# Moving conv inputs to an idle GpSimd and projection ahead of conv, in a kernel of attention and dynamic filters

## Chip, cores, metric

One core of one Trainium2 chip. The metric is the device time of one execution in microseconds (us), the median of several executions. A ratio is the mean time of one kernel's fast runs over the mean of the other's fast runs of the same rounds, so it is not quite the ratio of the medians quoted beside it. The call that a difference of two per cent is "faster" or "slower" uses a 95% interval.

## The reference

Four images of 256 channels, 48 x 48 pixels, fp32. Cut to what matters:

```python
# layer 0: group norm -> 3x3 conv 256->256 -> batch norm, relu -> q,k,v -> attention (8 heads,
# 2304 tokens) -> projection
x = x + _L0_conv_ref(_gn(x), ...)

# layer 1: group norm -> guidance -> five dynamic branches -> 1x1 conv -> batch norm
def _L1_conv_ref(x, W_cat, W_scale, gamma, beta):
    guidance = _conv(x, W_cat, pad=1)                       # 45 channels
    outs = [x]
    for i, d in enumerate((1, 6, 12, 24, 36)):
        w = softmax(guidance[:, 9*i : 9*(i+1)], axis=1)
        outs.append(_dyn_branch(x, w, d))                   # 9 shifted taps, each weighted per pixel
    y = _conv(concatenate(outs, axis=1), W_scale, pad=0)
    return (y - mean) * rsqrt(var + EPS) * gamma + beta     # mean, var over batch and pixels
x = x + _L1_conv_ref(_gn(x), ...)
```

## The kernel before

The 3x3 conv is computed in a transformed form: for each of six indices `i` a transformed weight `u_i` and a transformed input; the image is worked on in two halves `g`. The inputs come in three stages (0: indices 1 and 2; 1: indices 3 and 4; 2: indices 0 and 5). The conv is a generator that yields after each matmul, so other parts of the kernel can use it as filler: `run(n)` issues conv work worth `n`. This fixes the program order on every engine.

```python
        ORDER = (1, 2, 3, 4, 0, 5)
        ...
            def inputs(stage, g):                       # all on DVE
                ...
                if stage == 0:
                    for h in range(NH):
                        axpy(v4[5][:, h], d[2][:, h], -4.0, d[4][:, h])
                        axpy(v4[0][:, h], d[1][:, h], -4.0, d[3][:, h])
                    tt(v[1], v[5], v[0], ALU.add)
                    tt(v[2], v[5], v[0], ALU.subtract)
                elif stage == 1: ...
            ahead = weights(ORDER[0])
            for at, i in enumerate(ORDER):
                u = ahead
                if at + 1 < len(ORDER):
                    ahead = weights(ORDER[at + 1])
                for g in range(2):
                    if at == 0:
                        inputs(0, g)
                    if at in (1, 3):
                        inputs((at + 1) // 2, g)
                    for o in range(NH):
                        ...  # six matmuls, yield after each, then outputs(i, g, o, m)
```

The joint phase of image b (dynamic filters of b, conv and q/k/v of b + 1 as filler) opens so:

```python
            run(3500)                                   # conv work first
            while chunk < NCK:
                project(b, chunk, ao, ..., norm)        # projection of attention, norm statistics
                chunk += 1
            run(3000)
            for _ in norm.finish(misc):                 # small steps of the norm
                run(1500)
            for h in range(NH):
                normalize(inside(gn, h), inside(gn, h), norm.mean, norm.rstd, h)
                run(2000)
            for got in weights(0):                      # guidance, softmax, transposes
                if not got:
                    run(1300)
            # then the taps, with conv and q/k/v as filler
```

## Time and profile before

| | before |
|---|---|
| time, median (range) | 3212.65 us (3209.42 to 3214.46, 4 runs) |
| first conv matmul | 37.0 us |
| end of the first conv with q/k/v | 156.4 us |
| opening of a joint phase: last attention sums to first tap (three of them) | 67.21, 67.09, 67.15 us |
| tap stage after it | 297.0, 296.4, 294.3 us |

How to read the rows: a joint phase begins for us where TensorE forms the last sums of the softmax ("den") of the attention before it. "pg" is the guidance conv, "wb" the first tap, "pc" a conv matmul, "pp" the projection. The opening is den to first wb, and it has two halves, den to pg and pg to wb.

The table of stretches for the two halves of the first opening, kernel before; columns as the prediction gives them (length, busy time and instructions of PE, weight load, DVE, ACT, POOL, clock, DMA share, GB/s):

```profile
555.70:589.90 34.20, 24.16 (x86) 16.76 (x86) 16.20 (x35) 3.08 (x6) 0.00 (x0) 0.80 0.25 81
589.90:622.90 33.00, 33.00 (x165) 21.07 (x165) 13.98 (x27) 5.10 (x10) 0.00 (x0) 1.00 0.09 26
```

In the first half TensorE idles for 10 us; in the second it has no gap at all. GpSimd does nothing in either.

### The profile page before, as it was taken

How to read it: one execution, taken by the hardware profiler on the slowest of the kernel's cores; microseconds unless marked ns; L12 is line 12 of the kernel's file. 1: busy time of each engine (PE TensorE's matmuls, PEld its weight loads, DVE VectorE, ACT ScalarE, POOL GpSimd, SP SyncE). 2: the span in 40 equal slices, each digit the busy share in tenths (PEclk: the TensorE clock that was granted, in tenths of full speed). 3: DMA queues.
4: the chain of work that ended last, by engine and by line, in shares of the span. 5: the costliest groups of instructions: out<-in, count | busy, mean ns of one | idle time of the engine just before them, and what ended most of it. 6: DMA issues, size and time to landing. Idle time of an engine off the chain costs nothing.

```text
span 3208.1 us, 42897 instructions
## 1 busy us (share of the span) xinstructions
PE 2892.8 (90%) x17494; PEld 1301.4 (41%) x17494; DVE 2441.5 (76%) x2422; ACT 1514.4 (47%) x1724; POOL 1005.5 (31%) x752
## 2 busy tenths in 40 slices
PE   5999999979899999898999999987989999978873
PEld 4722223555542223455562222455554222334441
DVE  5488888487768888668767888848776888858785
ACT  0388877111148888301117887711114888840002
POOL 4000000189940000058980000018894000007672
PEclk9999999999999999999999999999999999988876
DMA  3400000100030000100003000010001000040005
GB/s 147 98 1 6 6 11 8 58 25 20 10 69 6 6 1 11 40 25 32 23 6 65 6 6 11 6 55 15 10 6 40 6 6 1 11 158 5 10 10 212
DMA packets 74701, 100.25 MB, mean 31 GB/s; under 512 B 51952, under 2 KB 62720, under 8 KB 71424
## 3 DMA queue, kind: packets, MB, share of 16 engines
q1 hardware_dynamic: 73696, 92.02, 9.8%
q0 software_dynamic: 800, 5.41, 0.4%
q8 instruction: 139, 2.28, 0.3%
q14 instruction: 66, 0.54, 0.1%
HBM read 64.39 MB, written 33.03 MB: 30 GB/s over the span
## 4 chain that ended last, share of the span: by engine, by line
PE 72%; DVE 12%; POOL 6%; ACT 4%; issue 4%; DMA 2%; SPq 0%; DVEq 0%; POOLq 0%; ACTq 0%
PE se L852 21%; PE num L882 18%; PE py L1141 10%; PE pc L766 7%; POOL cat L1225 6%; PE pg L1024 5%; DVE prod L1222 4%; PE wb L1201 3%; PE den L904 3%; ACT p L861 3%; PE pq L794 2%; PE pp L953 2%; DVE acc L897 2%; PE pv L813 1%; DVE yt L723 1%
## 5 line engine op out<-in xcount | busy, mean ns | idle before, releaser
L1225 POOL TENSOR_TENSOR cat<-cat,prod 128x752 f32<-128x752 f32 (+8 forms) x720 | 971.8, 1358 | 2113.7 <-DVE prod L1222 1155.5
L861 ACT ACTIVATE p<-se 128x1024 f32<-128x1024 f32 x1296 | 1259.0, 1026 | 282.2 <-PE se L852 243.8
L897 DVE TENSOR_TENSOR acc<-acc,p 128x2048 f32<-128x2048 f32 x504 | 1154.6, 2291 | 113.5 <-ACT p L861 74.7
L852 PE MATMUL se<-q,k 32*128 32x512 f32 (+1 forms) x5760 | 803.8, 594 | 12.0 <-ACT p L861 8.8
L1222 DVE TENSOR_TENSOR prod<-wb,pad 128x768 f32<-128x768 f32 (+7 forms) x768 | 551.6, 746 | 203.7 <-PE wb L1201 135.7
L882 PE MATMUL num<-p,vT 128*32 128x512 f32 (+1 forms) x5760 | 696.4, 563 | 8.8 <-ACT no L900 7.4
L1201 PE MATMUL wb<-w,pick 90*128 90x384 f32 (+3 forms) x888 | 434.4, 530 | 98.1 <-DVE prod L1222 86.8
L852 PEld LDWEIGHTS se<-q,k 32*128 32x128 f32 x5760 | 291.3, 183 | 529.0 <-issue 425.4
L1141 PE MATMUL py<-cat,wsc 128*128 128x384 f32 x960 | 397.0, 543 | 43.0 <-POOL cat L1225 43.0
L882 PEld LDWEIGHTS num<-p,vT 128*32 128x32 f32 x5760 | 121.7, 108 | 488.4 <-issue 440.2
L1201 PEld LDWEIGHTS wb<-w,pick 90*128 90x128 f32 x888 | 176.7, 203 | 261.9 <-DVE prod L1222 150.2
L1141 PEld LDWEIGHTS py<-cat,wsc 128*128 128x128 f32 x960 | 197.5, 212 | 152.0 <-POOL cat L1225 52.6
L766 PE MATMUL pc<-cv_q,u 128*128 128x288 f32 x576 | 165.1, 426 | 36.8 <-DMA u<-u_d 21.8
L766 PE MATMUL pc<-cv_k,u 128*128 128x288 f32 x576 | 164.0, 422 | 8.8 <-DVE cv_k L695 8.7
L1024 PE MATMUL pg<-pad,wcat 128*45 128x384 f32 x864 | 153.9, 499 | 2.6 <-DVE pad L582 2.4
L1216 DVE TENSOR_TENSOR cat<-wb,pad 128x768 f32<-128x768 f32 x114 | 108.2, 949 | 45.5 <-PE wb L1201 45.5
L766 PEld LDWEIGHTS pc<-cv_q,u 128*128 128x128 f32 x576 | 112.5, 201 | 69.9 <-issue 41.3
L794 PE MATMUL pq<-hid,wqkv 128*128 128x384 f32 x384 | 136.1, 486 | 0.0
L897 DVE TENSOR_TENSOR acc<-p,p 128x2048 f32<-128x2048 f32 x36 | 82.5, 2292 | 66.1 <-ACT p L861 66.1
L1156 ACT COPY y<-py 128x768 f32<-128x768 f32 x24 | 19.2, 798 | 231.5 <-PE py L1141 231.5
L766 PEld LDWEIGHTS pc<-cv_k,u 128*128 128x128 f32 x576 | 110.3, 197 | 37.9 <-issue 10.0
L710 ACT ACTIVATE hid<-yt,bn_t_f,bn_s 128x288 f32<-128x288 f32 x64 | 39.7, 626 | 167.7 <-DVE yt L728 97.7
(161 smaller groups left out, 1524.7 us busy)
## 6 DMA issues: line engine op xcount, KB each, us to landing
pad<-in_x SPq DMA_DIRECT2D x14, 1152.0 KB, 15.0
u<-u_d SPq DMA_DIRECT2D x18, 768.0 KB, 4.4
x_d<-pad SPq DMA_DIRECT2D x48, 192.0 KB, 2.5
y_d<-y SPq DMA_DIRECT2D x24, 384.0 KB, 2.7
xst<-in_x SPq DMA_DIRECT2D x36, 192.0 KB, 2.4
u_d<-u SPq DMA_DIRECT2D x6, 768.0 KB, 3.7
y<-y_d SPq DMA_DIRECT2D x2, 2304.0 KB, 13.8
x<-x_d SPq DMA_DIRECT2D x2, 2304.0 KB, 21.4
```

The source lines that it names most:

```text
L766: nc.tensor.matmul(m, u[:, h, kx, o * P : (o + 1) * P], halves[g][:, h, place[i], :, kx : kx + WW], start=(h == 0 and kx == 0), stop=(h == ...
L794: nc.tensor.matmul(pq[:, :CH], wqkv[:, i, s, g * P : (g + 1) * P], hid[:, i, cols], start=(i == 0), stop=(i == NH - 1),)
L852: nc.tensor.matmul(ss[j // 2][:, j % 2, at : at + n], k_[r, g, m * P : (m + 1) * P], q[r, g, q0 : q0 + n], start=True, stop=True,)
L861: nc.scalar.activation(p[:, 2 * pair : 2 * pair + 2, :], ss[pair], AF.Exp, scale=QS)
L882: nc.tensor.matmul(st["num"][r, at : at + n], vT[:, m, g * P + j * D : g * P + (j + 1) * D], p[:, j, at : at + n], start=(m == 0 and not s ...
L897: nc.vector.tensor_tensor(st["acc"], other, p, ALU.add)
L1024: nc.tensor.matmul(pg[64 * s : 64 * s + NG, :CH], wcat[:, i, k, :], window(gn, i, (c + s) * R, k // 3 - 1, k % 3 - 1), start=(i == 0 and k ...
L1141: nc.tensor.matmul(py[c][:, o, :CH], wsc[:, n * NH + i, o * P : (o + 1) * P], rhs(i), start=(n == 0 and i == 0), stop=(last and i == NH - 1),)
L1201: nc.tensor.matmul(pw[:, : nr * WW], pick[:, k : k + 1].to_broadcast([2 * NG, P]), w[:, l0 * WW : l1 * WW], start=True, stop=True,)
L1216: nc.vector.tensor_tensor(accv, wb, src, ALU.mult)
L1222: nc.vector.tensor_tensor(pv, wb, src, ALU.mult)
L1225: eng.tensor_tensor(dst, dst, pv, ALU.add)
```

## The change

Its intent: let the idle GpSimd make the conv inputs in the openings; put projection and norm, which lead to the guidance, ahead of the conv filler; load conv weights ahead of need; let DVE instead of GpSimd make the transformed weights at the start; take the norm's small steps off DVE. The diff, cut to its core:

```diff
 class Norm: finish()
-                nc.vector.tensor_copy(mean, pm[:, :NH])
-                nc.vector.tensor_tensor(d2, mv[:, :, 0], mean, ALU.subtract)
-                nc.vector.tensor_tensor(d2, d2, d2, ALU.mult)
-                nc.vector.tensor_tensor(d2, d2, mv[:, :, 1], ALU.add)
+                nc.scalar.copy(mean, pm[:, :NH])
+                for h in range(NH):
+                    nc.scalar.activation(d2[:, h : h + 1], mv[:, h, 0:1], AF.Square,
+                                         bias=mean[:, h : h + 1], scale=-1.0)
                 yield
-                nc.tensor.matmul(pv[:, :NH], gmat, d2, start=True, stop=True)
+                nc.tensor.matmul(pv[:, :NH], gmat, mv[:, :, 1], start=True, stop=False)
+                nc.tensor.matmul(pv[:, :NH], gmat, d2, start=False, stop=True)
 transformed weights, made once (made_from)
-                eng = nc.gpsimd          # eng.tensor_tensor(...)
+                nc.vector.tensor_tensor(...)
 conv inputs
+                tt = (nc.vector if b == 0 else nc.gpsimd).tensor_tensor
+                mul = nc.scalar.mul
                 if stage == 0:
-                    (four fused multiply-adds, two adds, on DVE)
+                    mul(v[0], d[2], 4.0)
+                    mul(v[5], d[1], 4.0)
+                    tt(v[0], d[4], v[0], sub)
+                    tt(v[5], d[3], v[5], sub)
+                    tt(v[1], v[0], v[5], add)
+                    tt(v[2], v[0], v[5], sub)
                 elif stage == 1:
+                    tt(v[6], d[3], d[1], sub)
+                    tt(v[5], d[4], d[2], sub)
+                    mul(v[6], v[6], 2.0)
+                    tt(v[3], v[5], v[6], add)
+                    tt(v[4], v[5], v[6], sub)
                 else:
+                    tt(v[0], d[0], d[2], sub)
+                    mul(v[6], v[6], 2.0)
+                    mul(v[0], v[0], 4.0)
+                    tt(v[0], v[0], v[5], add)
+                    tt(v[5], d[5], d[3], sub)
+                    tt(v[5], v[5], v[6], sub)
 when the inputs are issued: {(position in ORDER, half): [(stage, half)]}
+            if b == 0:
+                when = {(at, g): [(j, g)] for j, at in enumerate((0, 1, 3)) for g in range(2)}
+            else:
+                when = {(0, 0): [(0, 0)], (0, 1): [(0, 1), (1, 0), (1, 1)],
+                        (1, 0): [(2, 0), (2, 1)]}
 opening of a joint phase
-            run(3500)
             while chunk < NCK:
                 project(...)
             run(3000)
-            for _ in norm.finish(misc):
-                run(1500)
+            for at, _ in enumerate(norm.finish(misc)):
+                run((600, 1500)[at])
             for h in range(NH):
                 normalize(inside(gn, h), inside(gn, h), norm.mean, norm.rstd, h)
-                run(2000)
+            run(3500)
             for got in weights(0):
                 if not got:
-                    run(1300)
+                    run(800)
```

Left out: the first weights of the next conv are loaded before the joint phase begins, and the last phase keeps one tile in a buffer that has become free.

More of the change, by code (lines that the diff above doesn't have):

```diff
@@ L528, in conv_preact_kernel @@
         name="act", bufs=1
-    ) as act, tc.manual_schedule():
+    ) as act, tc.tile_pool(name="u", bufs=2) as upool, tc.manual_schedule():
         def image_of(src, b):
@@ L607, in finish, with shift_of @@
                 nc.tensor.matmul(pm[:, :NH], gmat, mv[:, :, 0], start=True, stop=True)
-                nc.vector.tensor_copy(mean, pm[:, :NH])
-                nc.vector.tensor_tensor(d2, mv[:, :, 0], mean, ALU.subtract)
-                nc.vector.tensor_tensor(d2, d2, d2, ALU.mult)
-                nc.vector.tensor_tensor(d2, d2, mv[:, :, 1], ALU.add)
+                nc.scalar.copy(mean, pm[:, :NH])
+                for h in range(NH):
+                    nc.scalar.activation(
+                        d2[:, h : h + 1], mv[:, h, 0:1], AF.Square, bias=mean[:, h : h + 1],
+                        scale=-1.0,
+                    )
                 yield
                 pv = psum_tile(f"pv_{self.name}")
-                nc.tensor.matmul(pv[:, :NH], gmat, d2, start=True, stop=True)
+                nc.tensor.matmul(pv[:, :NH], gmat, mv[:, :, 1], start=True, stop=False)
+                nc.tensor.matmul(pv[:, :NH], gmat, d2, start=False, stop=True)
                 rstd_of(rstd, pv[:, :NH])
                 self.mean, self.rstd = mean, rstd
+            def shift_of(self):
                 self.shift = small.tile([P, NH], F32, tag="gshift", name=f"gshift_{self.name}")
                 nc.vector.scalar_tensor_tensor(
-                    out=self.shift, in0=mean, scalar=-1.0, in1=rstd, op0=ALU.mult, op1=ALU.mult
+                    out=self.shift, in0=self.mean, scalar=-1.0, in1=self.rstd, op0=ALU.mult,
+                    op1=ALU.mult,
                 )
@@ L634, in conv_preact_kernel, with taken @@
         TN = TJ * WW
-        def taken_from(pool):
-            def load(i):
-                u = pool.tile([P, NH, 3, C], F32, tag="u", name=f"u_{i}")
-                nc.sync.dma_start(out=u, in_=u_d[i])
-                return u
-            return load
+        def taken(i):
+            u = upool.tile([P, NH, 3, C], F32, tag="u", name=f"u_{i}")
+            nc.sync.dma_start(out=u, in_=u_d[i])
+            return u
         def made_from(wc, pool):
             w = [wc[:, :, 3 * j : 3 * j + 3, :] for j in range(3)]
-            t = pool.tile([P, NH, 3, C], F32, tag="ut", name="u_t")
+            t = pool.tile([P, NH, 3, C], F32, tag="ut", name="u_t", bufs=1)
             def make(i):
-                u = pool.tile([P, NH, 3, C], F32, tag="u", name=f"u_{i}")
-                eng = nc.gpsimd
+                u = upool.tile([P, NH, 3, C], F32, tag="u", name=f"u_{i}")
                 if i == 1:
-                    eng.tensor_tensor(t, w[0], w[2], ALU.add)
+                    nc.vector.tensor_tensor(t, w[0], w[2], ALU.add)
                 if i == 3:
-                    eng.tensor_scalar(t, w[0], 0.25, None, ALU.mult)
-                    eng.tensor_tensor(t, t, w[2], ALU.add)
+                    nc.vector.tensor_tensor(t, w[0], w[2], ALU.add)
+                if i in (1, 3):
+                    nc.vector.tensor_tensor(u, t, w[1], ALU.add)
+                if i in (2, 4):
+                    nc.vector.tensor_tensor(u, t, w[1], ALU.subtract)
+                if i == 2:
+                    nc.scalar.mul(w[0], w[0], 0.25)
                     nc.scalar.mul(w[1], w[1], 0.5)
-                if i in (1, 3):
-                    eng.tensor_tensor(u, t, w[1], ALU.add)
-                if i in (2, 4):
-                    eng.tensor_tensor(u, t, w[1], ALU.subtract)
                 if i == 0:
-                    nc.scalar.mul(u, w[0], -1.5)
+                    nc.scalar.mul(u, w[0], -6.0)
                 if i == 5:
@@ L669, in made_from, with conv @@
             return make
-        def conv(b, gn, psum_tile, weights, pool, hid):
+        def conv(b, gn, psum_tile, weights, ready, pool, hid):
             halves = [
-                act.tile([P, NH, 6, TJ, PADW], F32, tag=tag, name=f"cv_{b}_{tag}")
+                act.tile([P, NH, 7, TJ, PADW], F32, tag=tag, name=f"cv_{b}_{tag}")
                 for tag in ("q", "k")
@@ L678, in conv @@
             S12, D12, S34, D34 = range(4)
-            place = {1: 1, 2: 2, 3: 3, 4: 4, 0: 1, 5: 2}
             def inputs(stage, g):
-                v = [halves[g][:, :, i].rearrange("p h t w -> p h (t w)") for i in range(6)]
-                v4 = [halves[g][:, :, i] for i in range(6)]
+                v = [halves[g][:, :, i] for i in range(7)]
                 d = [
@@ L687, in inputs @@
                 ]
-                tt, stt = nc.vector.tensor_tensor, nc.vector.scalar_tensor_tensor
-                def axpy(out, x, a, y):
-                    stt(out=out, in0=x, scalar=a, in1=y, op0=ALU.mult, op1=ALU.add)
+                tt = (nc.vector if b == 0 else nc.gpsimd).tensor_tensor
+                mul = nc.scalar.mul
+                add, sub = ALU.add, ALU.subtract
                 if stage == 0:
-                    for h in range(NH):
-                        axpy(v4[5][:, h], d[2][:, h], -4.0, d[4][:, h])
-                        axpy(v4[0][:, h], d[1][:, h], -4.0, d[3][:, h])
-                    tt(v[1], v[5], v[0], ALU.add)
-                    tt(v[2], v[5], v[0], ALU.subtract)
-                elif stage == 1:
-                    tt(v4[5], d[4], d[2], ALU.subtract)
-                    tt(v4[0], d[3], d[1], ALU.subtract)
-                    axpy(v[3], v[0], 2.0, v[5])
-                    axpy(v[4], v[0], -2.0, v[5])
-                else:
-                    tt(v4[1], d[0], d[2], ALU.subtract)
-                    axpy(v[1], v[1], 4.0, v[5])
-                    tt(v4[2], d[5], d[3], ALU.subtract)
-                    axpy(v[2], v[0], -4.0, v[2])
+                    mul(v[0], d[2], 4.0)
[4 more added lines that the diff above has]
+                    tt(v[2], v[0], v[5], sub)
+                elif stage == 1:
+                    tt(v[6], d[3], d[1], sub)
[3 more added lines that the diff above has]
+                    tt(v[4], v[5], v[6], sub)
+                else:
+                    tt(v[0], d[0], d[2], sub)
[4 more added lines that the diff above has]
+                    tt(v[5], v[5], v[6], sub)
             def relu(g, o, r, y):
@@ L749, in outputs @@
                     result(3, m, None, d12)
-            ahead = weights(ORDER[0])
+            if b == 0:
+                when = {(at, g): [(j, g)] for j, at in enumerate((0, 1, 3)) for g in range(2)}
+            else:
+                when = {
+                    (0, 0): [(0, 0)], (0, 1): [(0, 1), (1, 0), (1, 1)], (1, 0): [(2, 0), (2, 1)]
+                }
+            ahead = ready
             for at, i in enumerate(ORDER):
                 u = ahead
-                if at + 1 < len(ORDER):
-                    ahead = weights(ORDER[at + 1])
                 for g in range(2):
-                    if at == 0:
-                        inputs(0, g)
-                    if at in (1, 3):
-                        inputs((at + 1) // 2, g)
+                    for stage, gg in when.get((at, g), ()):
+                        inputs(stage, gg)
+                    if g == 0 and at + 1 < len(ORDER):
+                        ahead = weights(ORDER[at + 1])
                     for o in range(NH):
@@ L768, in conv @@
                                     u[:, h, kx, o * P : (o + 1) * P],
-                                    halves[g][:, h, place[i], :, kx : kx + WW],
+                                    halves[g][:, h, i, :, kx : kx + WW],
                                     start=(h == 0 and kx == 0),
@@ L776, in conv, with conv_qkv @@
                         yield MM * TN / CH
-        def conv_qkv(b, gn, psum_tile, weights, pool):
+        def conv_qkv(b, gn, psum_tile, weights, ready, pool):
             hid = keep("h", f"hid_{b}")
-            yield from conv(b, gn, psum_tile, weights, pool, hid)
+            yield from conv(b, gn, psum_tile, weights, ready, pool, hid)
             q, k_ = keep("q", f"q_{b}"), keep("k", f"k_{b}")
@@ L1288, in merged @@
                 pass
+        u_next = None
         for b in range(B + 1):
@@ L1302, in conv_preact_kernel @@
                 if b < B:
-                    if b == 0:
-                        for _ in norm0.finish(psc):
-                            pass
-                        for h in range(NH):
-                            normalize(inside(pads[0], h), rows_of(x_first[:, h, :]), norm0.mean,
-                                      norm0.rstd, h)
-                    weights = taken_from(work1)
+                    weights = taken
                     if b == 0:
@@ L1319, in conv_preact_kernel @@
                         weights = made_from(wc, work1)
+                        rest = norm0.finish(psc)
+                        next(rest)
+                        u_next = weights(ORDER[0])
+                        for _ in rest:
+                            pass
+                        for h in range(NH):
+                            normalize(inside(pads[0], h), rows_of(x_first[:, h, :]), norm0.mean,
+                                      norm0.rstd, h)
                     nn, stats = None, iter(())
@@ L1324, in conv_preact_kernel @@
                     other = merged(
-                        conv_qkv(b, pads[b % 2], psc, weights, work1), 40000.0, 4000.0,
+                        conv_qkv(b, pads[b % 2], psc, weights, u_next, work1), 40000.0, 4000.0,
                         stats,
@@ L1361, in conv_preact_kernel @@
                 load_pad(b + 1)
+                u_next = taken(ORDER[0])
                 fin = [None]
@@ L1368, in step @@
                         )
-                    next(fin[0], None)
+                    if next(fin[0], fin) is fin:
+                        nn.shift_of()
                 def piece(h, r0, b=b, nn=nn):
@@ L1392, in conv_preact_kernel @@
         with tc.tile_pool(name="last", bufs=1) as last:
-            t = [last.tile([P, NH, N], F32, tag=f"last{j}", name=f"last{j}") for j in range(3)]
-            nc.sync.dma_start(out=t[2], in_=y_d[B - 2])
-            again[B - 2] = t[2], again[B - 2][1]
+            t = [last.tile([P, NH, N], F32, tag=f"last{j}", name=f"last{j}") for j in range(2)]
+            nc.sync.dma_start(out=t[1], in_=y_d[B - 2])
+            again[B - 2] = t[1], again[B - 2][1]
+            t[1] = pads[(B - 1) % 2].rearrange("p h r w -> p h (r w)")
             for o in range(NH):
                 nc.sync.dma_start(out=t[0][:, o], in_=y_d[B - 1, :, o])
-                nc.sync.dma_start(out=t[1][:, o], in_=x1_d[B - 1, :, o])
+                nc.sync.dma_start(out=t[1][:, o, :N], in_=x1_d[B - 1, :, o])
             again.append(tuple(t[:2]))
```

## The prediction

> **What bounds the kernel now.** I read the table of stretches first, then the timeline of two openings, then who waits for whom. The timeline shows this course: a first conv (0 to 157 us), then four times attention (about 400 us) and a joint phase. Three joint phases (555 to 921 us is the first) run the dynamic filters of one image beside the conv and q/k/v of the next; the fourth has no conv; a store-bound tail of 48 us ends the run. Columns: length, then busy time (and instructions) of PE, weight load, DVE, ACT, POOL, clock, DMA share, GB/s.
> ```profile
> 37.00:157.00 120.00, 119.64 (x459) 88.28 (x459) 53.45 (x103) 36.03 (x60) 6.87 (x2) 1.00 0.36 86
> 157.00:555.00 398.00, 390.89 (x3148) 119.15 (x3148) 338.84 (x197) 328.04 (x350) 0.00 (x0) 1.00 0.03 6
> 555.70:623.00 67.30, 57.26 (x252) 37.93 (x252) 30.18 (x61) 8.18 (x16) 0.00 (x0) 0.90 0.17 54
> 623.00:921.00 298.00, 263.71 (x986) 164.59 (x984) 222.27 (x327) 38.12 (x65) 260.84 (x192) 0.95 0.06 20
> ```
> Attention is bound by TensorE (98%), and the change hardly touches it. The opening of a joint phase (third row) has an idle GpSimd and a TensorE that is busy 57 of 67 us; the stage of taps (fourth row) has TensorE at 88% and GpSimd at 88%, neither alone the bound. So the change can act on three things: the 37 us before the first conv matmul, three openings of 67 us, and three tap stages of 298 us.
>
> The start, from the timeline:
> ```profile
> 14.41 3.42 POOL L653 TENSOR_TENSOR u_t<-wc 128x1536 f32<-128x1536 f32 x1 [6.34 <-DMA wc<-in_conv_w]
> 15.49 2.36 DVE L609 TENSOR_TENSOR gd_n<-mvn,gmean_n 128x2 f32<-128x2 f32 x1
> 18.08 3.27 DVE L611 TENSOR_TENSOR gd_n<-gd_n,mvn 128x2 f32<-128x2 f32 x1
> 24.64 6.64 DVE L582 TENSOR_SCALAR pad<-x_first,gmean_n,grstd_n 128x2304 f32<-128x2304 f32 x2
> 31.20 4.82 DVE L690 SCALAR_TENSOR_TENSOR cv_q<-pad 128x300 f32<-128x300 f32 x4
> ```
> DVE operations on two elements per partition last 2.36 and 3.27 us here, and 0.16 us in the joint phase. L609 ends at 17.85 us, when the GpSimd instruction that began at 14.41 us ends: DVE waits for GpSimd, instruction by instruction.
>
> An opening, from the timeline of the first joint phase:
> ```profile
> 558.71 0.76 DVE L921 TENSOR_TENSOR ao<-no,rt 128x256 f32<-128x256 f32 x2
> 563.90 6.12 PE L766 MATMUL pc<-cv_q,u 128*128 128x288 f32 x16 [7.12 <-DMA u<-u_d]
> 569.86 2.74 PE L953 MATMUL pp<-ao,wp 128*128 128x384 f32 x8
> 585.90 1.48 DVE L582 TENSOR_SCALAR pad<-pad,gmean_n,grstd_n 128x2304 f32<-128x2304 f32 x1
> 589.94 11.82 PE L1024 MATMUL pg<-pad,wcat 128*45 128x384 f32 x72
> 622.94 0.56 PE L1201 MATMUL wb<-w,pick 90*128 90x384 f32 x1
> ```
> TensorE waits 7.1 us for conv weights, then runs almost without a gap to the first tap (wb, 622.9 us): 75 conv matmuls (two profile instructions each, 0.5 us a matmul when warm), projection and guidance.
>
> **What the Trainium skill says.** "SBUF — State Buffer", section "Who interferes with whom": a DVE instruction with two SBUF inputs, or in its 2-port mode, and a GpSimd instruction that reads SBUF exclude each other for a whole instruction. The trace agrees, as the 2.36 and 3.27 us above show; so it will again when GpSimd makes conv inputs. "GPSIMD Engine Reference", section 3.1, gives an add of 2048 fp32 elements 4497 ns there and 2293 ns on DVE; here 128x768 takes 1823 ns on GpSimd, 128x576 1406 ns, and a DVE add of 128x2048 2291 ns, which agrees. "TensorE: Matmul & The Clock Gate", section "What's actually happening", says that the matmul clock halves after about 3.4 us of idleness: the 16 instructions after the 7.1 us wait took 0.38 us each against 0.25 us, and the clock column is 0.90, so new gaps cost twice.
>
> **The change, part by part.**
>
> 1. First conv. DVE makes the transformed weights and GpSimd is idle at the start. Statistics are ready at 14.6 us as before. DVE: two adds of 1536 elements, by the slope of 2291 ns for 2048 some 1.75 us each, to 18.2 us; mean and squares run on ScalarE beside them; rstd to 18.85; two normalizations of 1.48 us (the uncontended time) to 21.9; two ScalarE scalings of 0.7 us, the first alone ahead of the DVE (1.49 us for 1536 elements and about 0.2 us fixed give 0.7 for 600); three adds of 0.78 us: first matmul at 25.2 instead of 37.0 us, 11.8 us earlier. After that the stretch is TensorE-bound, but the inputs of the second half now begin with ScalarE scalings that stand behind the evictions of the first half's result (the order of instructions shows it): 0.4 + 0.7 + 3 x 0.78 = 3.5 us of TensorE wait, and about 1 us for a PSUM buffer behind the six weight combinations that DVE now makes. Net -7 us.
>
> 2. Openings, up to guidance. The weights are fetched early: the 4.4 us between ao (559.5) and the first matmul (563.9) go. But GpSimd starts its adds (600 elements, 1.43 us between the two rows above) during the last steps of attention, and the two ao products have two SBUF inputs: about +2.5 us. Projection then starts near 561, statistics near 567, and twelve conv matmuls are done near 572. Now the order of instructions on ScalarE and TensorE decides. All inputs of the second half and of stage 1 are queued there: ScalarE's scaling for half two of stage 1 waits for the ninth GpSimd add (9 x 1.45 = 13 us), and the norm's square root stands behind that scaling; on TensorE pv stands behind the thirteenth conv matmul, which waits for the third of these adds. So: 572 + 0.4 (eviction) + 1.4 (scalings; the adds start after the first) + 13 + 0.7 (scaling) + 1.3 (table load) + 0.4 (root, reciprocal) = 588.5 to 589; normalization behind one GpSimd add, and guidance at about 591, against 589.9 before. Gain: none (+1 us).
>
> 3. Openings, guidance to first tap. Before: 601.8 to 622.9 us, 21 us, filled by 42 conv matmuls. After: 27 matmuls (13.5 us), but the exponential stands on ScalarE behind a stage-2 scaling that waits for five GpSimd adds: 3.4 + 4 x 1.45 + 0.7 + 1.3 + 0.4 = 11.6 us, then 4 to 5 us of DVE and transposes and evictions: about 18 us. Gain 3 us.
>
> 4. Tap stages. 75 - 49 = 26 conv matmuls, 13 us of TensorE, move from each opening into the stage of taps. It had 298 - 264 = 34 us of TensorE idleness, much of it waits on DVE or GpSimd, so I let 60% be absorbed: +5 us. The stage-2 inputs of half two (658.06 to 663.3 us, with waits for GpSimd) leave a DVE that is busy 83 to 92% in the three 20 us stretches from 643 to 703 us: -3 us.
>
> 5. Norm in attention and last joint phase, tail: some 0.2 us ScalarE operations instead of DVE ones; the tail is bound by the stores. 0.
>
> Sum: -7 + 3 x (1 - 3 + 5 - 3) = -7 us. The numbers in the new code (600, 1500, 3500, 800) look tuned for a gain, and my ScalarE-behind-GpSimd chains are the least certain steps, so I put the centre lower, at 3200 us (-14).
>
> **Rivals.** (a) The chain through ScalarE is shorter than I think, or other work fills it, and the taps absorb the moved matmuls: each opening ends 10 us earlier (26 matmuls less, minus 3), 3 x 10 + 7 = 37 us, giving 3177. For it: GpSimd idle in the openings (0.00 in the third row), TensorE idle 34 us in the taps. Against it: the order of instructions. (b) The openings stay as long and the tap stages, with TensorE and GpSimd both near 88%, take all 13 us: 3 x 12 - 7 = +29, giving 3243. For it: two engines near 90% with short buffers between them. Against it: early in that stage DVE is the busiest, and it is relieved. (c) Port waits between GpSimd's 24 adds and DVE stretch the openings further, 5 us each, on top of the central case: 3215. (d) Only the start matters, joints even: 3207.
>
> **Range and chances.** The rivals span 3177 to 3243; with (b) in its full size unlikely I take 3166 to 3232 for 8 in 10. Faster by over 2% needs 64 us, more than the start (12 us) and (a) yield together. Slower by over 2% would need 24 us in each joint phase. Faster 0.06, within 2% 0.91, slower 0.03.
>
> **What would show it.** In the new profile: first conv matmul near 25 us and attention from about 150 us (step 1); projection ahead of conv, a TensorE wait of about 5 us for a GpSimd add near the thirteenth matmul, and the norm's root idle until a scaling that waited for GpSimd (step 2); guidance 33 to 36 us after the last attention sums (34.2 before: 555.7 to 589.9); an exponential waiting behind scalings (step 3); tap stages longer by 0 to 6 us at a higher TensorE share (step 4). Wrong if openings shrink by over 6 us each, if tap stages do not lengthen or lengthen by the full 13 us, or if attention changes length.

## The result and the profile after

| | before | after |
|---|---|---|
| median (range), 4 runs each | 3212.65 us (3209.42 to 3214.46) | 3206.53 us (3203.57 to 3208.03) |
| ratio | | 0.9981, 95% interval 0.9964 to 0.9998: the same within 2% |

The change is worth 0.2%. Where the time of the two profiled executions (3208.1 and 3204.9 us, 3.1 us apart before rounding) went, from the start times in the two timelines:

| stretch | before | after | difference |
|---|---|---|---|
| start to end of first conv | 156.4 | 152.0 | -4.4 |
| first attention | 399.3 | 401.8 | +2.4 |
| three openings | 201.5 | 203.6 | +2.1 |
| three tap stages | 887.8 | 886.4 | -1.4 |
| attentions 2 to 4 | 1199.6 | 1196.4 | -3.1 |
| last joint phase and tail | 363.6 | 364.8 | +1.3 |

No row is large. The first conv starts 12 us earlier and ends only 4.4 us earlier. From the timeline of the start of the kernel after (start, length, engine, line, operation, out<-in, count, idle time before and its releaser):

```profile
14.70 1.70 DVE L657 TENSOR_TENSOR u_t<-wc 128x1536 f32<-128x1536 f32 x1
18.74 2.87 DVE L582 TENSOR_SCALAR pad<-x_first,gmean_n,grstd_n 128x2304 f32<-128x2304 f32 x2
24.79 8.16 PE L778 MATMUL pc<-cv_q,u 128*128 128x288 f32 x24 [8.01 <-DVE cv_q L699]
33.28 0.71 ACT L695 ACTIVATE cv_k<-pad 128x600 f32<-128x600 f32 x1
36.46 9.12 PE L778 MATMUL pc<-cv_k,u 128*128 128x288 f32 x24 [3.51 <-DVE cv_k L699]
```

The normalizations take 2.87 us for two where they took 6.64 beside a busy GpSimd. The second half's scaling on ScalarE (L695) starts only at 33.28, so TensorE waits 3.51 us and then runs 24 instructions at 0.38 us each in the mean instead of 0.25. In the trace the first twelve or so start 0.48 us apart and the rest 0.24: a cold clock, at half speed.

The two halves of the first opening and the tap stage, table of stretches, kernel after:

```profile
553.70:586.90 33.20, 18.94 (x64) 12.27 (x64) 9.24 (x15) 5.81 (x12) 22.30 (x16) 0.77 0.13 36
586.90:621.30 34.40, 30.79 (x138) 17.38 (x138) 10.35 (x17) 6.50 (x11) 14.17 (x9) 0.87 0.07 23
621.30:917.00 295.70, 265.84 (x1034) 171.21 (x1032) 222.56 (x324) 39.19 (x68) 260.11 (x192) 0.98 0.07 23
```

There are 49 TensorE instructions fewer in the opening (251 and 202), its TensorE busy time fell by 7.4 us (24.16 + 33.00 to 18.94 + 30.79), DVE's by a third, and yet it is as long as before: what was freed became idle time. Why, the timeline of the same stretch tells:

```profile
574.14 1.33 PE L778 MATMUL pc<-cv_k,u 128*128 128x288 f32 x2 [5.35 <-POOL cv_k L699]
576.15 0.16 DVE L84 TENSOR_SCALAR grstd_n<-pv_n 128x2 f32<-128x2 f32 x1 [10.65 <-PE pv_n L618]
582.75 0.70 ACT L704 ACTIVATE cv_k<-cv_k 128x600 f32<-128x600 f32 x1 [5.09 <-POOL cv_k L702]
583.47 1.28 ACT L85 ACT_TABLE_LOAD   x1
584.76 0.20 ACT L85 ACTIVATE grstd_n<-grstd_n 128x2 f32<-128x2 f32 x1
585.00 0.17 DVE L86 RECIPROCAL grstd_n<-grstd_n 128x2 f32<-128x2 f32 x1 [8.68 <-ACT grstd_n L85]
586.94 14.41 PE L1036 MATMUL pg<-pad,wcat 128*45 128x384 f32 x72 [5.56 <-DVE pad L582]
610.79 0.70 ACT L710 ACTIVATE cv_k<-cv_k 128x600 f32<-128x600 f32 x1 [5.57 <-POOL cv_k L708]
612.80 0.43 ACT L1067 ACTIVATE e<-e 128x270 f32<-128x270 f32 x1
615.63 2.83 PE L778 MATMUL pc<-cv_k,u 128*128 128x288 f32 x6 [3.58 <-DVE cs L745]
```

The norm's root (L85) needs only a 0.16 us DVE step, which ends at 576.31. It runs at 584.76, because the scaling L704 stands before it in ScalarE's queue and waits for GpSimd until 582.75. The reciprocal shows this as 8.68 us of waiting for ScalarE. Guidance then runs cold: 14.41 us for the 72 instructions that took 11.82. The exponential (612.80) stands in the same way behind a stage-2 scaling (L710) that waited 5.57 us for GpSimd. So the readings that the experiments have to test are: (T1) the opening is set by these two places where a ScalarE instruction of the norm or the softmax is queued behind a scaling that waits for GpSimd; rivals: (T2) GpSimd is too slow or collides with DVE, and the same inputs on DVE would be faster; (T3) the opening is set by the filler that is left in it; (T4) other parts of the change (weights at the start, norm steps) gained or lost what is missing.

### The profile page after: what moved, and what is told of

Same layout as the page of the kernel before. It is cut to its first block, busy times and chain, and to the rows that moved or that the text cites. A ratio compares the mean times of both kernels' runs of the same rounds, so it can differ in the third digit from the quotient of the medians.

```text
span 3204.9 us, 42929 instructions
## 1 busy us (share of the span) xinstructions
PE 2891.4 (90%) x17510; PEld 1305.2 (41%) x17510; DVE 2392.6 (75%) x2303; ACT 1547.3 (48%) x1789; POOL 1089.2 (34%) x817
## 4 chain that ended last, share of the span: by engine, by line
PE 68%; POOL 11%; DVE 10%; ACT 5%; issue 4%; DMA 1%; SPq 0%; POOLq 0%; DVEq 0%; ACTq 0%
PE se L864 21%; PE num L894 18%; POOL cat L1236 9%; PE py L1152 9%; PE pg L1036 5%; PE pc L778 4%; DVE prod L1233 3%; PE den L916 3%; PE wb L1212 3%; ACT p L873 3%; PE pq L806 2%; PE pp L965 2%; DVE acc L909 2%; PE pv L825 1%; DVE yt L730 1%
## 5 line engine op out<-in xcount | busy, mean ns | idle before, releaser
L864 PE MATMUL se<-q,k 32*128 32x512 f32 (+1 forms) x5760 | 804.5, 593 | 11.6 <-ACT p L873 8.5
L1152 PE MATMUL py<-cat,wsc 128*128 128x384 f32 x960 | 384.8, 529 | 43.5 <-POOL cat L1236 43.5
L778 PE MATMUL pc<-cv_k,u 128*128 128x288 f32 x576 | 174.2, 437 | 31.6 <-POOL cv_k L699 16.0
L1036 PE MATMUL pg<-pad,wcat 128*45 128x384 f32 x864 | 162.3, 521 | 19.3 <-DVE pad L582 19.0
## 6 DMA issues: line engine op xcount, KB each, us to landing
x<-x_d SPq DMA_DIRECT2D x2, 2304.0 KB, 21.2
```

Of the source, the lines that this page charges most:

```text
L778: nc.tensor.matmul(m, u[:, h, kx, o * P : (o + 1) * P], halves[g][:, h, i, :, kx : kx + WW], start=(h == 0 and kx == 0), stop=(h == NH - 1 ...
L864: nc.tensor.matmul(ss[j // 2][:, j % 2, at : at + n], k_[r, g, m * P : (m + 1) * P], q[r, g, q0 : q0 + n], start=True, stop=True,)
L1036: nc.tensor.matmul(pg[64 * s : 64 * s + NG, :CH], wcat[:, i, k, :], window(gn, i, (c + s) * R, k // 3 - 1, k % 3 - 1), start=(i == 0 and k ...
L1152: nc.tensor.matmul(py[c][:, o, :CH], wsc[:, n * NH + i, o * P : (o + 1) * P], rhs(i), start=(n == 0 and i == 0), stop=(last and i == NH - 1),)
```

## The experiments

Ten kernels ran, all with correct results; three rounds each. The kernel before measured 3208.17 us in the group of experiments 1, 3, 4 and 5, 3209.37 in that of stage 1 of experiment 2 and experiments 6, 7 and 8, and 3209.17 in that of stage 2 of experiment 2 and experiment 9. The changed kernel was not run again in these groups, so it is compared by ratios, each to the kernel before of its own rounds. I compare openings in the traces as well, since their three repetitions agree within about 0.8 us, while times of one kernel spread over 2 to 7 us.

### 1. Both doublings as GpSimd adds

```diff
-                    mul(v[6], v[6], 2.0)              # stage 1, ScalarE
+                    tt(v[6], v[6], v[6], add)         # GpSimd, for b > 0
-                    mul(v[6], v[6], 2.0)              # stage 2
-                    mul(v[0], v[0], 4.0)
+                    tt(v[6], v[6], v[6], add)
+                    tt(v[0], v[0], v[0], add)
+                    tt(v[0], v[0], v[0], add)
```

This gives GpSimd more work, and takes from ScalarE every instruction that waits for GpSimd's results of stages 1 and 2.

> The changed kernel, but in the joint phases the five scalings that wait for a GpSimd result (one of v6 in stage 1, one of v6 and one by four of v0 in stage 2, each for two halves) are made by GpSimd itself as additions of a value to itself, so that nothing on ScalarE waits for GpSimd between the first half's eviction and the exponential. Theory (the opening is held by ScalarE standing behind GpSimd, and the taps absorb the moved conv matmuls): guidance starts about 5 us earlier against the last attention sums (28 instead of 33.2 us), runs warm (12 instead of 14.4 us), first tap about 12 us earlier (55 instead of 67.5 us), tap stage still about 298 us, so each joint phase is 10 to 12 us shorter and the kernel 30 to 36 us faster than the changed one (ratio to before near 0.988). Rival (a joint phase is set by its total TensorE and GpSimd work, and what the opening saves the taps take back): first tap earlier, tap stage longer by about as much, total within 5 us of the changed kernel.

Measured: 3163.41 us (3159.69 to 3165.46), ratio to before 0.9859 (0.9842 to 0.9875). Guidance starts 28.50, 28.22 and 28.05 us after the last sums (33.2 to 33.6 in the changed kernel), the first tap 54.94, 54.74 and 54.61 us after them (67.5 to 68.1). Timeline of the first opening of this kernel:

```profile
574.19 1.33 PE L786 MATMUL pc<-cv_k,u 128*128 128x288 f32 x2 [5.35 <-POOL cv_k L699]
576.40 0.20 ACT L85 ACTIVATE grstd_n<-grstd_n 128x2 f32<-128x2 f32 x1 [4.62 <-DVE grstd_n L84]
581.66 11.82 PE L1044 MATMUL pg<-pad,wcat 128*45 128x384 f32 x72
598.41 0.43 ACT L1075 ACTIVATE e<-e 128x270 f32<-128x270 f32 x1 [1.54 <-DVE e L1071]
```

The root now waits for nothing but its own DVE step, guidance runs warm, the exponential follows its data. GpSimd has eight adds more per image than in the changed kernel, and each opening is 13 us shorter: T1 holds. By ratio the kernel is 39 us faster than the changed one, a little more than I expected. The wait of 5.35 us ahead of the second half's first matmul is still there.

### 2. One doubling at a time

The first kernel changes stage 1 alone, the second stage 2 alone:

```diff
 first kernel
-                    mul(v[6], v[6], 2.0)              # stage 1
+                    tt(v[6], v[6], v[6], add)         # for b > 0
 second kernel
-                    mul(v[6], v[6], 2.0)              # stage 2
-                    mul(v[0], v[0], 4.0)
+                    tt(v[6], v[6], v[6], add)         # for b > 0
+                    tt(v[0], v[0], v[0], add)
+                    tt(v[0], v[0], v[0], add)
```

> The changed kernel with only the stage-1 scalings (those ahead of the norm's root on ScalarE) made by GpSimd. Theory (two separate chains of ScalarE behind GpSimd): guidance at 28 instead of 33.2 us after the last attention sums and 12 instead of 14.4 us long, but the exponential still waits for stage 2, so that first tap comes near 58 to 60 instead of 67.5 us; joint phases 7 to 9 us shorter, kernel 22 to 28 us faster than the changed one. Rival (one common cause, as GpSimd's amount of work): no more than half of the gain of both, under 19 us.

> Stage 1 keeps its ScalarE scaling, stage 2 doubles by GpSimd adds. Two separate chains: the stage-1 scaling holds the norm's root, so guidance should start 33.0 to 33.6 us after the last attention sums as in the changed kernel; the stage-2 scalings no longer hold the exponential, so guidance to first tap should shrink from 34.4 us by the 6 us that the two chains of the double version left over after the stage-1 version. First tap near 61 to 62 us, time near 3186 us. If both scalings form one chain of which the first is the cause, the first tap stays at 67 to 68 us and the time near 3205.

| | guidance after last sums | first tap after last sums | median | ratio to before |
|---|---|---|---|---|
| stage 1 alone | 28.15 to 28.47 | 60.88 to 61.26 | 3184.99 | 0.9927 (0.9911 to 0.9944) |
| stage 2 alone | 33.23 to 33.31 | 62.05 to 62.14 | 3184.90 | 0.9926 (0.9909 to 0.9942) |
| both | 28.05 to 28.50 | 54.61 to 54.94 | 3163.41 | 0.9859 (0.9842 to 0.9875) |

The two places are separate and nearly add up: stage 1 gives 6.8 us per opening (67.9 less 61.1, means), stage 2 gives 5.8, both give 13.1. For stage 1 alone I had expected the first tap at 58 to 60 us; it came at 61, and by ratio the kernel is 17 us faster than the changed one, under the 19 us that I had set as the mark of the rival, a single common cause. Stage 2 alone speaks against that rival: it too gives GpSimd more adds, leaves guidance where it was and still gains nearly as much. With stage 2 alone the timeline shows GpSimd's doublings (the first of three here) and the exponential right behind its data:

```profile
599.37 1.20 POOL L713 TENSOR_TENSOR cv_k<-cv_k 128x600 f32<-128x600 f32 x1
603.05 1.46 POOL L716 TENSOR_TENSOR cv_k<-cv_k 128x600 f32<-128x600 f32 x1
604.84 0.43 ACT L1072 ACTIVATE e<-e 128x270 f32<-128x270 f32 x1 [1.00 <-DVE e L1068]
```

### 3. The inputs on DVE

```diff
-                tt = (nc.vector if b == 0 else nc.gpsimd).tensor_tensor
+                tt = nc.vector.tensor_tensor
```

> The changed kernel with the conv inputs of the joint phases back on DVE (0.78 instead of 1.45 us an addition), all else as changed. Theory: the chain of nine additions ahead of the norm's root is 7 instead of 13 us, the four ahead of the exponential 3 instead of 6, and no port waits on the last attention products (2.89 back to 0.76 us), so guidance is 5 to 7 us and the first tap 8 to 10 us earlier than in the changed kernel, tap stage unchanged, total 20 to 28 us faster than the changed kernel. Rival: GpSimd frees DVE for something that matters, then the total is the same or slower.

Measured: 3208.19 us (3203.78 to 3210.42), ratio 0.9997 (0.9981 to 1.0014). My expectation failed: an add that takes 0.78 us instead of 1.45 did not shorten anything. Guidance starts 34.49 to 34.77 us after the last sums, the first tap 67.4 to 67.7. Timeline of the first opening:

```profile
578.09 0.56 PE L618 MATMUL pv_n<-gd_n,gmat 128*128 128x2 f32 x2
582.42 0.78 DVE L706 TENSOR_TENSOR cv_k<-cv_k 128x600 f32<-128x600 f32 x1
583.11 0.15 DVE L84 TENSOR_SCALAR grstd_n<-pv_n 128x2 f32<-128x2 f32 x1
605.98 0.78 DVE L713 TENSOR_TENSOR cv_k<-cv_k 128x600 f32<-128x600 f32 x1
606.68 0.43 DVE L1058 COPY e<-pt 128x270 f32<-128x270 f32 x1
```

The norm's variance is ready at 578.65, but its DVE step runs at 583.11, right behind the last add of stage 1; the softmax's copy runs right behind the last add of stage 2. The scalings stayed on ScalarE, and its scaling and table load ahead of the root end only at 582.95. So the root is now held by both queues, DVE's and ScalarE's, and TensorE's first conv matmul also waits 4.62 us for DVE's adds. T2 falls in the form "the same inputs on DVE would be faster"; together with experiment 1, where GpSimd does more adds and the opening is shorter, the slower add by itself doesn't explain the opening.

### 4. More filler in the second half of the opening

```diff
-                    run(800)
+                    run(1300)
```

> The changed kernel with the old 1300 instead of 800 as the conv budget of each small step of the first weights, so about 14 conv matmuls (7 us) go back from the tap stage into the opening. If the tap stage absorbs conv matmuls without growing (as the trace of the changed kernel says, 298 us both before and after), the opening grows by 4 to 6 us, the tap stage stays, and the kernel is 12 to 18 us slower than the changed one. If the tap stage is bound by TensorE, it shrinks by what the opening grows, and the total is the same within 4 us.

Measured: 3193.94 us (3193.90 to 3195.88), ratio 0.9957 (0.9940 to 0.9973). Neither branch of what I expected came: it is not slower and not the same within 4 us, but some 8 us faster (ratios 0.9957 and 0.9981, each to the kernel before of its own rounds; the three joint phases are 2.8 us shorter each, 360.5 against 363.3 in the mean). Table of stretches, second half of the opening and tap stage:

```profile
583.90:619.90 36.00, 35.95 (x166) 21.65 (x166) 10.10 (x18) 7.22 (x13) 14.43 (x9) 0.92 0.13 44
619.90:911.00 291.10, 263.80 (x1006) 168.44 (x1004) 219.99 (x322) 38.39 (x66) 259.32 (x192) 0.96 0.07 21
```

28 more instructions, some 7 us of warm TensorE, lengthen the half by only 1.6 us, since TensorE had idled 3.6 us there and now not at all, and its clock is a little higher. They leave the tap stage, which shortens by 4.3 us (295.7 to 291.4, mean of the three 291.2 against 295.5). So the tap stage is partly bound by TensorE, and T3 in the form "the opening is as long as its filler" is wrong for the changed kernel: its opening was waiting.

### 5. Weights at the start on GpSimd again

```diff
-                    nc.vector.tensor_tensor(u, t, w[1], ALU.add)       # and the other three
+                    nc.gpsimd.tensor_tensor(u, t, w[1], ALU.add)
```

> The changed kernel with the weight combinations at the start back on GpSimd (in the new order and with the new scalings). Theory of the start (GpSimd's additions of 1536 elements, 3.4 us each, shut DVE out of the shared SBUF port): the normalizations take more than 1.48 us each and the first conv matmul is at 28 to 31 us instead of 24.8. Norm steps on ScalarE are no longer shut out, so less is lost than in the kernel before (37.0). Later weights come 3.4 us a piece but beside DVE. Total 3 to 6 us slower than the changed kernel. Rival: the order alone (weights of the first step ahead of the norm, nothing else beside it) gave the gain, then the first matmul is within 1 us of 24.8.

Measured: 3209.00 us (3207.15 to 3213.76), ratio 1.0003 (0.9986 to 1.0020). The first conv matmul comes at 32.29 us instead of 24.79, and the first conv ends at 156.78 instead of 151.96. Timeline of the start:

```profile
16.64 6.82 DVE L582 TENSOR_SCALAR pad<-x_first,gmean_n,grstd_n 128x2304 f32<-128x2304 f32 x2
27.32 4.00 DVE L698 TENSOR_TENSOR cv_q<-pad,cv_q 128x600 f32<-128x600 f32 x1
```

A DVE add that takes 0.78 us alone takes 4.00 us beside GpSimd's, and the two normalizations 6.82 instead of 2.87. So the 4.8 us at the start belong to the weights' move to DVE (I had expected 28 to 31 us for the first matmul, so the loss is larger than I thought). The openings stay as they were, 67.8 to 68.2 us. In the total it is at the limit of what these rounds tell apart.

### 6. Norm steps on DVE again

The change in `finish()` undone, all else kept:

```diff
-                nc.scalar.copy(mean, pm[:, :NH])
-                (two squares on ScalarE, two matmuls for pv)
+                nc.vector.tensor_copy(mean, pm[:, :NH])
+                nc.vector.tensor_tensor(d2, mv[:, :, 0], mean, ALU.subtract)
+                nc.vector.tensor_tensor(d2, d2, d2, ALU.mult)
+                nc.vector.tensor_tensor(d2, d2, mv[:, :, 1], ALU.add)
+                (one matmul for pv)
```

> The changed kernel with the norm's small steps (mean, square, sum) back on DVE. If keeping them away from DVE spares port waits in the joint phases, guidance comes 1 to 4 us later and the kernel is 3 to 12 us slower. My reading of the trace: GpSimd stands idle for 10 us just then (559 to 570 us) and what follows is held by other things, so the joint phases stay within 0.5 us, and only the start loses about 1 to 2 us, because the steps stand behind the two weight combinations on DVE. Total within 4 us.

Measured: 3205.72 us (3201.14 to 3207.48), ratio 0.9990 (0.9974 to 1.0007). Guidance after 33.47 to 33.54 us and first tap after 67.9 to 68.0 us, as in the changed kernel; at the start the first conv matmul comes at 26.07 instead of 24.79. The root waits for the same scaling whoever makes the steps before it. With experiments 5 and 6, T4 is out as an explanation of the openings.

### 7. The start with both halves' inputs made early

```diff
-                when = {(at, g): [(j, g)] for j, at in enumerate((0, 1, 3)) for g in range(2)}
+                when = {(0, 0): [(0, 0), (0, 1)], (1, 0): [(1, 0)], (1, 1): [(1, 1)],
+                        (3, 0): [(2, 0)], (3, 1): [(2, 1)]}
```

> The changed kernel with the inputs of the second half of the first conv queued together with those of the first half, ahead of the first evictions on ScalarE. Theory: TensorE's wait of 3.5 us before the second half goes, and the 9.1 us of the second half's 24 matmul instructions become 6.0 (warm clock): first conv 5 to 7 us shorter, joint phases unchanged, kernel 5 to 7 us faster than the changed one. If the wait was not due to that order, no change.

Measured: 3200.48 us (3196.21 to 3200.97), ratio 0.9973 (0.9956 to 0.9989). The first conv ends at 144.65 us, 7.3 earlier than in the changed kernel. Timeline of the start:

```profile
24.41 8.05 PE L779 MATMUL pc<-cv_q,u 128*128 128x288 f32 x24 [8.43 <-DVE cv_q L699]
32.29 5.98 PE L779 MATMUL pc<-cv_k,u 128*128 128x288 f32 x24
```

With the second half's scalings ahead of the evictions, TensorE has no wait, and the second 24 instructions take 5.98 us instead of 9.12. The wait (3.5) and the cold clock (3.1) make up most of the 7.3 us. The total doesn't show the expected 5 to 7 us clearly: by ratio it is 2.6 us faster than the changed kernel, and the two intervals overlap.

### 8. All of it: doublings on GpSimd, both halves' inputs early in every conv

Experiments 1 and 7 together, and for the later images:

```diff
-                    (0, 0): [(0, 0)], (0, 1): [(0, 1), (1, 0), (1, 1)], (1, 0): [(2, 0), (2, 1)]
+                    (0, 0): [(0, 0), (0, 1)], (0, 1): [(1, 0), (1, 1)], (1, 0): [(2, 0), (2, 1)]
```

> Doublings by GpSimd as in the first experiment, and the inputs of the second half queued with those of the first, in the first conv and in the joint phases. Theory: TensorE's wait of 5.35 us for GpSimd's third addition of half two goes, pv comes earlier and with it the norm; guidance near 21 to 23 us after the last attention sums instead of 28.3, first tap near 48 to 50 instead of 54.8, tap stage 296, plus the 6 us of the first conv: 20 us faster than the kernel of the first experiment, near 3143. If another wait takes its place (the DVE normalization behind GpSimd), guidance near 26 and some 10 to 13 us.

Measured: 3135.82 us (3133.35 to 3138.64), ratio 0.9774 (0.9757 to 0.9790): faster than both kernels, 2.3% against before. Timeline of the first opening:

```profile
560.14 0.65 PE L787 MATMUL pc<-cv_k,u 128*128 128x288 f32 x2
562.05 0.21 ACT L85 ACTIVATE grstd_n<-grstd_n 128x2 f32<-128x2 f32 x1
565.05 11.82 PE L1045 MATMUL pg<-pad,wcat 128*45 128x384 f32 x72
591.87 0.55 PE L1221 MATMUL wb<-w,pick 90*128 90x384 f32 x1
```

The third wait of the opening, TensorE's 5.35 us for the second half's inputs, was in front of the norm's own small matmul in TensorE's queue. Without it guidance starts 19.86 to 20.46 us after the last sums (28 in experiment 1) and the first tap 46.7 to 46.8 us after them. That is 8.6 us in the first opening, more than the wait of 5.35. Most of the rest is the cold clock again, by the two timelines: guidance stands on TensorE right behind 16 conv instructions, which took 5.71 us after the wait and 4.13 without it; the two ahead of them took 1.33 and 0.65, and the projection 5.21 and 4.65. The tap stages stay at 293.0 to 296.0 us.

### 9. The same with more filler

The kernel of experiment 8 with

```diff
-                    run(800)
+                    run(1300)
```

> The best version so far (GpSimd doublings, early inputs) with the filler budget of 1300 for each weight computation in place of 800. If the tap stage is partly bound by TensorE, moving about 14 conv matmuls (7 us) out of it shortens it by the 4 us seen with the same edit on the changed kernel (295.7 to 291.4). In the opening TensorE has only few us of idleness left now, so it should grow by 3 to 7 us (46.5 to 50 to 53). Net between minus 1 and plus 3 us per joint phase: 3133 to 3145 us, against 3136 without. If the opening still has idle TensorE time as in the changed kernel, it is 3124 to 3128.

Measured: 3135.87 us (3133.13 to 3137.30), ratio 0.9771 (0.9755 to 0.9787), so no difference from experiment 8. In the first joint phase the opening grew from 46.7 to 54.3 us and the tap stage shrank from 296.0 to 288.7. Table of stretches, second half of the first opening, experiment 8 and then this one:

```profile
565.05:591.87 26.82, 26.38 (x138) 15.75 (x138) 11.31 (x17) 4.01 (x7) 26.11 (x19) 1.00 0.09 30
566.30:599.30 33.00, 33.00 (x167) 21.13 (x166) 10.35 (x18) 4.70 (x9) 24.86 (x18) 1.00 0.14 48
```

In experiment 8 TensorE already idled only 0.44 us there, against 3.6 in the changed kernel, so the added work lengthens the half by 6.2 us. The same edit that gained 8 us on the changed kernel gains nothing here: what leaves the tap stage comes back in full.

## Why the prediction was right

The total was right (3200 predicted, 3206.5 measured, in the range), and so was the call of "within 2%". Not every step had its size, and that the sum of the steps (-7) came so near is in part luck: in step 3 the three openings together came out 13 us longer than predicted, while steps 2 and 4 came out 5 and 7 us shorter, and these errors cancel. The lower centre (-14), put there for a look of tuning and not for a mechanism, was farther off than the sum.

**Step 1, the first conv: -7 predicted, -4.4 measured at its end.** The first matmul came at 24.79 (25.2 predicted) and the wait was 3.51 us (3.5 predicted). The term that failed is one that the sum did not have: after the wait the clock is cold, 9.12 instead of 5.98 us for 24 instructions, 3.1 us more. The prediction itself said that "new gaps cost twice" and then did not charge this gap. Experiment 7 removed both and gained 7.3 us. One profile is not exact to the microsecond here: experiments 1 to 4 have the same code up to this point, and their first conv ended at 150.5 to 151.5 us, against 152.0 in the changed kernel's profile. The first attention then lost another 2.4 us. In the kernel after its first sums run at a slow clock, here from its timeline:

```profile
159.46 1.94 PE L894 MATMUL num<-p,vT 128*32 128x512 f32 x8
```

The same eight instructions take 1.07 us in the kernel before, and some 2.2 us of the lead are lost within 12 us from there. The change is not the cause of that: in experiments 3, 4 and stage 1 of 2, with the same code up to there, these eight take 1.06 to 1.07 us, and in experiments 1 and stage 2 of 2 again 1.94. It differs from execution to execution; what decides it, no run here settles.

**Step 2, up to guidance: +1 predicted, -0.7 measured** (34.15 to 33.42, means of three). The mechanism is the predicted one, in order: TensorE waits 5.35 us near the thirteenth matmul, the root stands behind the scaling that waits for the ninth add, the normalization follows. (The terms of the prediction's sum add to 589.2, not 588.5 to 589.) The size was off at its beginning: projection began 4.4 us after the last sums, where 5.3 were reckoned. Experiments 1 and 2 show the mechanism: with the stage-1 scaling off ScalarE guidance comes 5 us earlier.

**Step 3, guidance to first tap: -3 predicted, +1.3 measured** (33.0 to 34.3 in the first phase; +1.4 in the mean of three). Two terms were mis-sized. Guidance itself took 14.41 instead of 11.82 us, cold after a TensorE wait of 5.56 us for the normalization: +2.6 that the sum lacked. The rest, end of guidance to first tap, went from 21.2 to 19.9 us, so -1.3 instead of -3: the exponential ended 11.9 us after guidance (11.6 predicted), but from there to the first tap it took 8.0 us and not 6.4. The queue behind the stage-2 scaling is shown by experiment 2.

**Step 4, tap stages: +2 net predicted, -0.5 measured** (mean of three). By the prediction's own list ("wrong if ... tap stages do not lengthen") this step failed. 52 instructions moved in, as predicted (26 matmuls). At 0.25 us they are 13 us of TensorE work, yet its busy time grew by 2.1 us (263.72 to 265.84), as the mean of one instruction fell from 0.269 to 0.257 us with the granted clock up from 0.95 to 0.98. That a denser TensorE keeps its clock is my reading; no run isolates it. The 60% that I let be absorbed was not free either: experiment 4 got 4.3 us back for 14 matmuls, 60% of their 7 us. So the charge for 26 would be about 8 us, not 5, and what offset it, perhaps fewer DVE operations and the clock, some 8 us and not 3. This split is worked out, not measured apart.

**Step 5, norm and last phase: 0 predicted, +1.3 measured.** Experiment 6 agrees for the norm steps: no effect in the openings. The last joint phase, which is the same code in all kernels after the change except for the norm steps of experiment 6, took 313.0 us in the changed kernel without the tail (before: 311.7), 309.8 to 310.8 in eight of the ten experiments, 313.1 in experiment 8 and 314.4 in experiment 3. So I take the 1.3 us there for the spread of executions. The same holds for attentions 2 to 4 (-3.1 us): in the ten experiments they took 1192.8 to 1200.5 us together, so their change doesn't count as the sign "wrong if attention changes length".

**Where the gain went.** The intent was sound: experiments 1 and 8 turn the same move into 45 and 74 us against the kernel before of their own rounds. It was lost because GpSimd's results were consumed on ScalarE, and TensorE, ahead of the norm and the softmax in program order. What the other parts of the change are worth by themselves, projection ahead of conv and the early loading of weights, no run here isolates. Of the rivals, (a), a gain of 10 us per opening, is what appears once those queues are cleared; it was not wrong about the idle time, only about its use. Rival (c), port waits, is visible in the trace but not what sets the opening: in experiment 3, with DVE alone and no such waits, it is no shorter.

## What to carry to other kernels

When work moves to an idle engine, look at who consumes its results, and at what stands behind that consumer in its own queue: one scaling on ScalarE that waits for GpSimd held back for 8 us a root that itself takes 0.2 us, and doing this scaling and the others of its kind on the slow engine itself, as adds, was worth 1.2% (ratio 0.9859 against 0.9981). A gap of 3 to 6 us in front of a block of matmuls should be charged twice, once as the wait and once as the cold clock after it (3.1 and 2.6 us here). And a filler budget should be tuned again after each such repair: the same number gained 8 us while TensorE idled in that half of the opening and nothing after.

## What the Trainium skill lacked or had wrong

- "PSUM — Partial Sum Buffer", section "Engine vs sequencer instructions", says that the queues of ScalarE, VectorE and GpSimdE are strictly first in, first out. The runs agree, but the page draws no cost from it: here it held a 0.20 us root for 8.5 us (data at 576.31, run at 584.76; a table load of 1.28 us lies within), and removing it was worth 6.8 us per opening.
- "ScalarE: Activation LUTs", section "What ACT_TABLE_LOAD costs", gives about 1283 ns for the load and a further 1380 ns for a drain. The load took 1.28 us here, but the root followed it by 0.01 us (583.47 + 1.28, root at 584.76): and it began 0.02 us after the scaling before it ended (582.75 + 0.70), so no drain shows on either side.
- "GPSIMD Engine Reference", section 3.1, gives one time for an add. Here an add of a 600-element operand to itself took 1.18 to 1.20 us (stage 2 alone, experiment 2), of two different operands mostly 1.35 to 1.48 us.
- On the port lock and the clock gate, the pages that the prediction cites agree with the runs (0.78 to 4.00 us for a DVE add beside GpSimd; matmul instructions that start 0.48 us apart after 3.5 us of waiting and 0.24 later).
